# Where the extra transpositions of an attention slot stand: behind the turns, or between the dense tile and the values

## The chip, the cores and the metric

The kernel runs on one core of a Trainium2 chip. The metric is the device time of one execution in microseconds; the kernel before took 3290.62 us, the median of three runs (3289.79 to 3292.32).

## What is computed

The input is 4 sequences of 2048 tokens of width 512, in float32. Two residual blocks follow each other:

```python
x = x + layernorm(attention(layernorm(x), w_qkv))
x = x + layernorm(ffn(layernorm(x), ...))
```

The attention has 16 heads of width 32 and is local: a window of 128 queries sees its own 128 keys, those before and those after (384 keys, 256 at the two ends of a sequence):

```python
qkv = x @ w_qkv
scores = einsum('bhnqe,bhnke->bhnqk', q * E**-0.5, k_ctx)   # k_ctx: three neighbouring windows
out = einsum('bhnqk,bhnke->bhnqe', softmax(scores), v_ctx)
```

The feed-forward block mixes its weights for each sequence: a gate `g` is the mean over the tokens of `relu(x @ gate_w1.T + gate_b1) @ gate_w2.T + gate_b2`, and `W1 + sum_e g[e] * TW1[e]` (the same for W2 and the biases) is what the sequence is multiplied with, with a tanh-approximated GELU between. Only the attention part is touched by the change.

## The kernel before

**Two stages.** The first stage runs the attention, makes the normalized tokens of the second block (`xn2`) and writes them transposed to DRAM, and computes the gate. The second stage runs the feed-forward block. The mixing of the weights (`mixer`) is spread over both: it loads expert weights on SP's DMA queue (tile `exps`, four buffers, three ahead) and adds each to an accumulator with one VectorE (DVE) instruction.

**Slots.** The first stage is a loop over 256 slots (`for i in range(NS)`). There are 64 windows `W_` of 128 tokens, 16 a sequence, and 4 groups `g` of four heads each; slot `i` is window `i // 4`, group `i % 4`. The program is scheduled by hand: each engine executes its instructions in the order in which the Python code emits them, and waits only for data and for free buffers. One slot emits in this order:

1. `scores(i + 1)`: the scores of the next slot (L517), and on DVE their row maxima `nm` (L526).
2. In some slots a "fore" tile: one product of the query, key and value projection (`product`, L450) with its evacuation (`produced`). The projection of a block of 512 tokens is done with a seven-product scheme, spread over 12 slots, even products in `dense`, odd ones in `fore`.
3. `turn(i, j)` for the three (at sequence ends two) key blocks: four transpositions of probabilities each (tile `ptp`, L554) into a PSUM buffer, and a copy by ScalarE (ACT) to `prT` (L556).
4. `exponentials(i + 1)` on ACT (L539), in slots with a fore tile half of them ahead of it.
5. The entries of `mid[i]`: before the change only `pto`, in slots with `i % 4 == 0`. `out_transposes` (L248) turns the output of the window before back to token order; `out_scaled` normalizes it on DVE.
6. The entries of `rest[i]` (loads on SP, statistics and normalizations on DVE and POOL, stores on SP) and, from slot 84 on, 0 to 3 steps of the mixer (loads and stores on SP, L144 on DVE). Nothing here runs on TensorE (PE) or ACT.
7. The dense tile of the slot: either a projection product as above (`pm`, L450, PSUM pool `ps_m` with one buffer), or, in slots 12 to 15 of each 16, a tile of the gate (`pmg`, L163, four matmuls of 512 columns) whose ReLU with a sum runs on ACT (L168), or near the end of the stage an early piece of the feed-forward block (`pme`, L693). Evacuations are on ACT or DVE.
8. The first entry of `aux[i]`.
9. `values(i)`: 12 products with the values (tile `po`, L570) and a copy by ACT to `oT` (L577).
10. The further entries of `aux[i]`, then `late[i]`.

**What stands in aux.** Two kinds of transposition, of four PE instructions and one ACT copy each. `place_tile` (tile `pt_a`, L370, copied to `xnT`, L371) turns the normalized input of a coming block, in slots 12 to 15 of each 16. `via_pt(xn2_transposes, xn2_store, ...)` (tile `ptx`, L277, copied to `xo`, L282) turns `xn2` of a finished window, followed by its DMA store to `xT_d` on SP (L283); it comes in slots 0, 4, 8 and 11 of each 16, and at the end of the stage also in other slots. In no slot does `aux` hold more than one entry.

**Buffers.** All transposition tiles and `po` come from one PSUM pool with three buffers:

```python
ps_t = actx.enter_context(tc.tile_pool(name="ps_t", bufs=3, space=PSUM))
```

They are handed out in turn, so a tile waits until the third tile before it has been copied out. In a slot with three turns, `pto` and one aux entry the sequence is turn 0, turn 1, turn 2, `pto`, aux, `po`: `pto` takes the buffer of turn 0, the aux tile that of turn 1, `po` that of turn 2.

Of the kernel before, what the change touches and what calls it, by code (L numbers as in the profile page):

```python
# [34 lines left out]
def sandwich(ctx: ExitStack, tc: tile.TileContext, x, w_qkv, gw1, gb1, gw2, gb2, w1, b1, w2, b2, tw1, tb1, tw2, tb2, out):  # L35
    nc = tc.nc
# [226 lines left out]
    def residual(W_):  # L263
        st = win[W_]
        x1 = st["x1"]
        normalize(x1, st["a"], st["sb"])
        nc.vector.tensor_tensor(x1, x1, st["x"], ALU.add)
        nc.sync.dma_start(x1_d[W_], x1)
        st["sc"] = stats(x1, f"c{W_}")

    def normed(W_):
        st = win[W_]
        normalize(st["xn2"], st["x1"], st["sc"])
# [48 lines left out]
    with ExitStack() as actx:  # L322
# [6 lines left out]
        def load_tile(K, t, tag, bufs):  # L329
            b, k = divmod(K, NBLK)  # L330
            xt = qkvp.tile([P, D], F32, tag=tag, bufs=bufs, name=f"{tag}_{K}_{t}")
            nc.sync.dma_start(xt, x[b, k * TB + t * P : k * TB + (t + 1) * P])
            return xt
# [23 lines left out]
        def norm_stats(K, t):  # L357
            xs_of[K, t] = stats(x_of[K, t], f"a{K}_{t}")

        def norm_tile(K, t):  # L360
            xn = xn_of[K, t] = x_of.pop((K, t))
            normalize(xn, xn, xs_of.pop((K, t)))

        def place_tile(K, t, evac):
            if t == 0:
                xnT_of[K] = qkvp.tile([P, KC, TB], F32, tag="xnT", bufs=2, name=f"xnT_{K}")
            pt = ps_t.tile([P, KC, P], F32, tag="pt", name=f"pt_a{K}_{t}")
            xn = xn_of.pop((K, t))
            for kc in range(KC):
                nc.tensor.transpose(pt[:, kc, :], xn[:, ts(kc, P)], ident)  # L370
            evac(xnT_of[K][:, :, ts(t, P)], pt)  # L371
# [39 lines left out]
        def right_factors(K, part):  # L411

            x = xnT_of[K]
            r11, r12, r21, r22 = (x[:, 2 * i : 2 * i + 2, j * Q : (j + 1) * Q] for i in range(2) for j in range(2))
            if part == 0:
                t = wp.tile([P, 3, 2, Q], F32, tag="tx", name=f"tx_{K}")
                rights[K] = {"11": r11, "21": r21, "22": r22, "T1": t[:, 0], "T2": t[:, 1], "T3": r12, "T4": t[:, 2]}
                nc.vector.tensor_tensor(t[:, 0], r12, r11, ALU.subtract)
                nc.vector.tensor_tensor(t[:, 1], r22, t[:, 0], ALU.subtract)
            else:  # L420
                t = rights[K]
                nc.vector.tensor_tensor(r12, r22, r12, ALU.subtract)
                nc.vector.tensor_tensor(t["T4"], r21, t["T2"], ALU.subtract)
# [14 lines left out]
        def product(K, i, u, half, key=0):  # L438
            l, r, begins, _, _ = products[u]
            if begins and half == 0 and key:  # L440
                sc = ps_s.tile([P, 2, TB], F32, tag="sc", name=f"pm_{K}_{i}_{u}")
                bank[key] = sc[:, 0, :].rearrange("p (a b) -> p a b", a=2)
            elif begins and half == 0:
                bank[0] = ps_m.tile([P, 2, Q], F32, tag="pm", name=f"pm_{K}_{i}_{u}")
            if u < 2 and half == 0:
                rights.setdefault(K, {"11": xnT_of[K][:, :2, :Q], "21": xnT_of[K][:, 2:, :Q]})
            left, right = lefts[i][l], rights[K][r]
            for kc in range(2):
                a, b = (left, right) if i < 2 else (right, left)
                nc.tensor.matmul(  # L450
                    bank[key][:, half, :],
                    lhsT=a[:, kc, ts(half, P)],
                    rhs=b[:, kc, :],
                    start=(begins and half == kc == 0),
                    stop=True,
                    skip_group_check=True,
                )

        def produced(K, i, u, key=0):
            d = (q_of, k_of, v_of)[i]  # L460
            if u == 0:
                d[K] = projection(K, i)
            _, _, _, (row, col), added = products[u]
            if i == 2:
                row, col = col, row
            to = d[K][:, 2 * row : 2 * row + 2, col * Q : (col + 1) * Q]
            if added and i == 0:
                nc.vector.scalar_tensor_tensor(to, bank[key], QSCALE, to, ALU.mult, ALU.add)
            elif added:
                nc.vector.tensor_tensor(to, bank[key], to, ALU.add)  # L470
            elif i == 0:
                (nc.vector.tensor_scalar_mul if u == 3 else nc.scalar.mul)(to, bank[key], QSCALE)
            elif u == 3:
                nc.vector.tensor_copy(to, bank[key])
            else:
                nc.scalar.copy(to, bank[key])
# [103 lines left out]
        slots = range(-16, NS + 64)  # L580
        fore = {i: None for i in slots}
        dense = {i: None for i in slots}
        aux = {i: [] for i in slots}
        rest = {i: [] for i in slots}
        first = {i: [] for i in slots}
        mid = {i: [] for i in slots}
        late = {i: [] for i in slots}
        for K in range(1, NBK):
            s0 = 4 * (4 * K - 5)
            if K > 1:  # L590
                for t in range(WB):

                    i = s0 - 14 + 4 * t if K > 2 else s0 + t - 3
                    rest[i - 2].append(lambda K=K, t=t: x_of.__setitem__((K, t), load_tile(K, t, "x", 4)))
                    rest[i].append(lambda K=K, t=t: norm_stats(K, t))
                    rest[i + 1].append(lambda K=K, t=t: norm_tile(K, t))
                    aux[s0 + t].append(lambda K=K, t=t: place_tile(K, t, nc.scalar.copy))
            for part in range(2):
                rest[s0 + 4 + part].append(lambda K=K, part=part: right_factors(K, part))
            for i in range(3):  # L600
                for u in range(7):

                    (fore if u % 2 else dense)[s0 + 4 + 4 * i + (u + 1) // 2] = (
                        lambda half, K=K, i=i, u=u: product(K, i, u, half),
                        lambda K=K, i=i, u=u: produced(K, i, u),
                    )
# [11 lines left out]
        def gate_tile(K, oc, half):  # L618
            if half == 0:
                bank[0] = ps_m.tile([P, TB], F32, tag="pm", name=f"pmg_{K}_{oc}")  # L620
            gate_matmuls(bank[0], gT_of[K], oc, range(2 * half, 2 * half + 2))

        gate_at = {K: 4 * (4 * (K + 3) - 5) for K in range(11)} | {11: 204, 12: 220, 13: 236, 14: 248}
        for K, s0 in gate_at.items():
            first[s0 - 2].append(lambda K=K: load_gate(K))
            for oc in range(KC):
                dense[s0 + oc] = (
                    lambda half, K=K, oc=oc: gate_tile(K, oc, half),
# [25 lines left out]
        def via_pt(fill, use, W_, tag):  # L654
            pt = ps_t.tile([P, KC, P], F32, tag="pt", name=f"{tag}_{W_}")
            fill(W_, pt)
            use(W_, pt)

        for W_ in range(NWA - 1):
            mid[4 * W_ + 4].append(lambda W_=W_: via_pt(out_transposes, out_scaled, W_, "pto"))  # L660
            rest[4 * W_ + 5].append(lambda W_=W_: residual(W_))
            rest[4 * W_ + 6].append(lambda W_=W_: normed(W_))

            i = 4 * W_ + 8 if W_ < 58 and W_ % WB != 1 else 4 * W_ + 7
            aux[i].append(lambda W_=W_: via_pt(xn2_transposes, xn2_store, W_, "ptx"))

        first[240].append(lambda: load_first(0, 0, 0, wp, "w2"))
        first[240].append(lambda: load_first(0, 0, 1, wp, "w3"))
# [91 lines left out]
        for i in range(NS):  # L760
            W_, g = divmod(i, KC)
            nk = span_of(W_)[1]
            for f in first[i]:
                f()
            if i + 1 < NS:
                scores(i + 1)
            more = i + 1 < NS
            if fore[i]:
                fore[i][0](0)
                fore[i][0](1)  # L770
                if more:
                    exponentials(i + 1, (0, 1))
                fore[i][1]()
            for j in range(nk):
                turn(i, j)
            if more:
                exponentials(i + 1, (2, 3) if fore[i] else range(4))
            for f in mid[i]:
                f()

            for f in rest[i]:
                f()
            if i >= 84:
                for _ in range(MIXED[i % 16]):
                    next(blend)
            if dense[i]:
                dense[i][0](0)
                dense[i][0](1)
                dense[i][1]()
            for f in aux[i][:1]:  # L790
                f()
            values(i)
            for f in aux[i][1:] + late[i]:
                f()


# [371 lines left out]
```

## Time and profile before

| | us |
|---|---|
| median of three runs | 3290.62 |
| the profiled execution | 3291.22 |
| its span, first to last instruction | 3289.3 |
| PE busy, whole span | 3259.1 |
| stretch 60 to 1710 us (attention slots) | 1650.00 |
| PE busy in it | 1643.72 |
| DVE busy in it | 1281.49 |
| ACT busy in it | 1188.84 |
| POOL busy in it | 265.90 |

The groups of instructions that matter for the slots:

| line, engine, tile | count | busy us | mean ns |
|---|---|---|---|
| L554 PE, ptp | 2944 | 372.3 | 276 |
| L570 PE, po | 5888 | 214.8 | 277 |
| L517 PE, sc | 2816 | 245.1 | 422 |
| L163 PE, pmg | 480 | 215.9 | 592 |
| L556 ACT, prT | 736 | 385.8 | 594 |
| L539 ACT, exponentials | 1024 | 574.9 | 583 |
| L526 DVE, maxima | 512 | 449.9 | 919 |
| L144 DVE, mixer | 512 | 687.1 | 1342 |

A PE instruction's duration is longer than the step from one start to the next, since matmuls are pipelined and their ends are modelled; what a group of PE work costs is read from the start of it to the start of the next. "Idle before" is the time in which the engine did nothing, with the instruction or DMA that ended it. A float32 matmul shows as two PE records, so a dense tile of four matmuls is x8 in the timeline; a transposition is one record.

### The profile page before, as it was taken

To read this page: it belongs to the slowest core of one execution; us is meant where nothing else is said; L and a number is where in the kernel's file an instruction comes from. 1 tells how busy PE (TensorE), PEld (TensorE's weight loads), DVE (VectorE), ACT (ScalarE), POOL (GpSimd) and SP (SyncE) were. 2 spreads that over 40 slices of the span, in tenths; PEclk is the share of its full clock that TensorE was granted. 3 is DMA by queue.
4 is the path that set the end of the run, shared out by engine and by line. 5 is a ranking of instruction groups with operands and counts; after the bars stand their busy time and mean duration, and the time that the engine had idled before them with its cause. 6 is when DMAs were issued, how large, how long until landed. Compare 5 with 4: busy or idle time off the path is not lost.

```text
span 3289.3 us, 58549 instructions
## 1 busy us (share of the span) xinstructions
PE 3259.1 (99%) x22886; PEld 2627.5 (80%) x22886; DVE 2074.1 (63%) x2887; ACT 1572.6 (48%) x4212; POOL 722.5 (22%) x840
## 2 busy tenths in 40 slices
PE   9999999999999999999999999999999999999998
PEld 7777777777777777777768888888888888888887
DVE  5656555888888888888874665566556656412221
ACT  3777777677776777777771221122222122222121
POOL 1111111122221122111112322332322333321222
PEclk9999999999999999999999999999999999999999
DMA  2111111556665566656677789978788888732332
GB/s 85 50 62 49 43 52 53 169 193 202 215 214 181 193 203 213 196 177 204 232 264 270 259 288 329 334 284 298 273 320 319 304 287 302 278 109 90 128 128 78
DMA packets 316118, 651.96 MB, mean 198 GB/s; under 512 B 22969, under 2 KB 89657, under 8 KB 295490
## 3 DMA queue, kind: packets, MB, share of 16 engines
q1 hardware_dynamic: 315842, 648.22, 57.2%
q8 instruction: 180, 2.95, 0.4%
q14 instruction: 96, 0.79, 0.1%
HBM read 538.03 MB, written 110.10 MB: 197 GB/s over the span
## 4 chain that ended last, share of the span: by engine, by line
PE 95%; DVE 1%; DMA 1%; ACT 1%; POOL 1%; issue 0%; SPq 0%; DVEq 0%; ACTq 0%; POOLq 0%
PE pm L450 18%; PE px L817 13%; PE ptp L554 10%; PE px L915 9%; PE pz L915 7%; PE sc L517 7%; PE pz L817 6%; PE pmg L163 6%; PE po L570 6%; PE py L915 3%; PE py L817 3%; PE py2b L915 3%; PE pto L248 1%; DMA exps<-in_tw 1%; PE ptx L277 1%; PE pt_a L370 1%
## 5 line engine op out<-in xcount | busy, mean ns | idle before, releaser
L144 DVE SCALAR_TENSOR_TENSOR acc<-exps,g,acc 128x1024 f32<-128x1024 f32 x512 | 687.1, 1342 | 185.5 <-DMA exps<-in_tw 179.6
L539 ACT ACTIVATE pr<-sc,nm 128x384 f32<-128x384 f32 (+1 forms) x1024 | 574.9, 583 | 218.3 <-DVE nm L526 218.3
L526 DVE TENSOR_REDUCE nm<-sc 128x2 f32<-128x768 f32 (+1 forms) x512 | 449.9, 919 | 279.7 <-PE sc L517 277.8
L556 ACT COPY prT<-ptp 128x512 f32<-128x512 f32 x736 | 385.8, 594 | 164.6 <-PE ptp L554 159.9
L994 ACT ACTIVATE y<-y,shift,rs_d 128x512 f32<-128x512 f32 x64 | 52.0, 813 | 742.8 <-POOL shift L993 742.8
L554 PEld LDWEIGHTS ptp<-ident,pr 128*128 128x128 f32 x2944 | 329.6, 141 | 54.2 <-issue 32.9
L554 PE MATMUL ptp<-ident,pr 128*128 128x128 f32 x2944 | 372.3, 276 | 0.0
L817 PE MATMUL px<-tT,w 128*128 128x256 f32 x1512 | 349.9, 379 | 1.9 <-ACT cpb L868 1.9
L817 PEld LDWEIGHTS px<-tT,w 128*128 128x128 f32 x1512 | 286.7, 190 | 42.4 <-ACT cpb L868 3.3
L517 PE MATMUL sc<-k,q 32*128 32x384 f32 (+2 forms) x2816 | 245.1, 422 | 5.2 <-ACT pr L539 5.0
L874 DVE TENSOR_TENSOR cpb<-pz,cpb 128x512 f32<-128x512 f32 x63 | 43.5, 691 | 326.3 <-PE pz L817 285.6
L92 POOL TENSOR_SCALAR ve_b<-mv_b 128x1 f32<-128x1 f32 x64 | 47.1, 737 | 837.8 <-DVE mv_b L90 837.8
L915 PE MATMUL px<-w2s,u 128*128 128x256 f32 x1024 | 228.9, 379 | 0.7 <-ACT last L282 0.7
L539 ACT ACTIVATION_READ_ACCUMULATOR pr<-sc,nm 128x1 f32 x1024 | 224.0, 219 | 0.0
L915 PEld LDWEIGHTS px<-w2s,u 128*128 128x128 f32 x1024 | 194.5, 190 | 27.3 <-ACT last L282 0.9
L163 PE MATMUL pmg<-gT,gw_sb 128*128 128x512 f32 x480 | 215.9, 592 | 0.0
L570 PE MATMUL po<-prT,v 128*32 128x128 f32 x5888 | 214.8, 277 | 0.1
L570 PEld LDWEIGHTS po<-prT,v 128*32 128x32 f32 x5888 | 145.3, 109 | 71.1 <-issue 56.8
L892 POOL TENSOR_TENSOR t<-u 128x512 f32<-128x512 f32 x64 | 84.0, 1312 | 503.0 <-ACT u L829 487.1
L450 PE MATMUL pm<-xnT,wqkv 128*128 128x256 f32 x744 | 183.3, 389 | 0.0
L517 PEld LDWEIGHTS sc<-k,q 32*128 32x128 f32 x2816 | 120.0, 183 | 60.7 <-issue 45.5
L450 PEld LDWEIGHTS pm<-xnT,wqkv 128*128 128x128 f32 x744 | 134.9, 191 | 41.6 <-ACT oT L577 22.3
(169 smaller groups left out, 5310.3 us busy)
## 6 DMA issues: line engine op xcount, KB each, us to landing
exps<-in_tw SPq DMA_DIRECT2D x512, 512.0 KB, 5.9
w2s<-m2d SPq DMA_DIRECT2D x112, 1024.0 KB, 6.4
acc<-in_w SPq DMA_DIRECT2D x64, 512.0 KB, 6.7
x<-in_x SPq DMA_DIRECT2D x64, 256.0 KB, 3.0
m1d<-acc SPq DMA_DIRECT2D x64, 256.0 KB, 6.1
m2d<-acc SPq DMA_DIRECT2D x64, 256.0 KB, 6.9
w<-m1d SPq DMA_DIRECT2D x16, 1024.0 KB, 8.2
fxT<-xTd SPq DMA_DIRECT2D x16, 1024.0 KB, 9.0
```

What stands on the lines that cost most here:

```text
L144: nc.vector.scalar_tensor_tensor(acc, ets.pop(n), g_all[b][:, e : e + 1], acc, ALU.mult, ALU.add)
L163: nc.tensor.matmul(pm, lhsT=gw1_sb[:, kc, ts(oc, P)], rhs=xT[:, kc, :], start=(kc == 0), stop=(kc == KC - 1))
L450: nc.tensor.matmul(bank[key][:, half, :], lhsT=a[:, kc, ts(half, P)], rhs=b[:, kc, :], start=(begins and half == kc == 0), stop=True, skip ...
L517: nc.tensor.matmul(scs[r // 2][:, r % 2, col : col + nj * W], lhsT=q[rows, g, ts(W_ % WB, W)], rhs=k_of[kb][rows, g, j0 * W : (j0 + nj) * ...
L526: nc.vector.tensor_reduce(st["nm"][:, h : h + 2], scs[u][:, :, : nk * W], AX.X, ALU.max, negate=True)
L539: nc.scalar.activation(pr[:, : nk * W], scs[r // 2][:, r % 2, : nk * W], AF.Exp, bias=st["nm"][:, h : h + 1], accum_out=st["den"][:, h : h ...
L554: nc.tensor.transpose(pt[:, r, :], st["pr"][g * 4 + r][:, ts(j, W)], ident)
L556: nc.scalar.copy(prT, pt)
L570: nc.tensor.matmul(po[r * E : (r + 1) * E, 0, :], lhsT=v_of[kb][:, jj, h * E : (h + 1) * E], rhs=prT[:, r, :], start=(j == 0), stop=(j == ...
L817: nc.tensor.matmul(bank[:, f, :], lhsT=factor[:, f, kc * P : (kc + 1) * P], rhs=right[:, kc, :], start=(start and f == 0 and kc == 0), sto ...
L892: nc.gpsimd.tensor_tensor(t1s[c], b12, us[c][:, :, :Q], ALU.subtract)
L915: nc.tensor.matmul(bank[:, t, :], lhsT=right(c - c % 2)[:, c % 2, ts(t, P)], rhs=w[:, c, :], start=(start and c == t == 0), stop=True, ski ...
```

## The change

The dictionary `aux` is gone. `place_tile` and the `xn2` transposition with its copy and its store now stand in `mid[i]`, so they are emitted after the turns and the exponentials, ahead of `rest[i]`, the mixer's steps and the dense tile. In slots that have `pto` as well, `pto` is put at the head of `mid[i]`, so it stays the first tile behind the turns. After the dense tile `values(i)` follows directly. The instructions are the same ones, and the three PSUM buffers are handed out in the same sequence.

```diff
-        aux = {i: [] for i in slots}
...
-                    aux[s0 + t].append(lambda K=K, t=t: place_tile(K, t, nc.scalar.copy))
+                    mid[s0 + t].append(lambda K=K, t=t: place_tile(K, t, nc.scalar.copy))
...
         for W_ in range(NWA - 1):
-            mid[4 * W_ + 4].append(lambda W_=W_: via_pt(out_transposes, out_scaled, W_, "pto"))
+            mid[4 * W_ + 4].insert(0, lambda W_=W_: via_pt(out_transposes, out_scaled, W_, "pto"))
             rest[4 * W_ + 5].append(lambda W_=W_: residual(W_))
             rest[4 * W_ + 6].append(lambda W_=W_: normed(W_))
 
             i = 4 * W_ + 8 if W_ < 58 and W_ % WB != 1 else 4 * W_ + 7
-            aux[i].append(lambda W_=W_: via_pt(xn2_transposes, xn2_store, W_, "ptx"))
+            mid[i].append(lambda W_=W_: via_pt(xn2_transposes, xn2_store, W_, "ptx"))
...
                 dense[i][0](0)
                 dense[i][0](1)
                 dense[i][1]()
-            for f in aux[i][:1]:
-                f()
             values(i)
-            for f in aux[i][1:] + late[i]:
+            for f in late[i]:
                 f()
```

On PE the moved transpositions pass the slot's dense tile. On ACT their copy passes the evacuation of the dense tile, where that is on ACT. On SP the store of `ptx` passes the DMAs that `rest[i]` and the mixer issue in that slot. On DVE and POOL the order is unchanged.

## The prediction

> **What bounds the kernel.** First the page's rows of busy time and the chain of work that ended last:
>
> ```profile
> PE 3259.1 (99%) x22886; PEld 2627.5 (80%) x22886; DVE 2074.1 (63%) x2887; ACT 1572.6 (48%) x4212; POOL 722.5 (22%) x840
> ...
> PE 95%; DVE 1%; DMA 1%; ACT 1%; POOL 1%; issue 0%; SPq 0%; DVEq 0%; ACTq 0%; POOLq 0%
> ```
>
> TensorE runs 3259.1 of 3289.3 us and is 95% of the chain. The table of stretches narrows it to where the diff acts: from 60 to 1710 us (the attention slots) PE is busy 1643.72 of 1650.00 us, ACT 1188.84, DVE 1281.49. So in these slots a nanosecond between the start of one PE group and the start of the next is a nanosecond of the kernel, and nothing else is, unless it makes PE wait. I therefore read PE's timeline, start to start. Columns: start, duration, engine, line, operation, tiles, shape, count.
>
> ```profile
> 1022.41 1.53 PE L554 MATMUL ptp<-ident,pr 128*128 128x128 f32 x12
> 1023.80 0.66 PE L248 MATMUL pto<-ident,oT 128*128 128x128 f32 x4
> 1024.30 1.89 PE L450 MATMUL pm<-xnT,wqkv 128*128 128x256 f32 x8
> 1026.03 0.60 PE L277 MATMUL ptx<-ident,x 128*128 128x128 f32 x4
> 1026.56 0.86 PE L570 MATMUL po<-prT,v 128*32 128x128 f32 x24
> ...
> 1030.04 1.47 PE L554 MATMUL ptp<-ident,pr 128*128 128x128 f32 x12
> 1031.35 1.89 PE L450 MATMUL pm<-tx,wsum 128*128 128x256 f32 x8
> 1033.17 0.86 PE L570 MATMUL po<-prT,v 128*32 128x128 f32 x24
> ```
>
> The second slot has no extra transposition: twelve turn transpositions take 1.31 us (0.109 each), the dense tile 1.82 up to the values. In the first slot, dense to ptx takes 1.73 and ptx to the values 0.53: together 2.26, that is 1.82 and 0.44, four times 0.109. **Where it stands now, the second transposition costs its bare 0.44 us.** The one behind the turns (pto) does not: turns to pto 1.39, pto to dense 0.50.
>
> **What such a place costs.** Two parts can be read off. The tile pto takes the PSUM buffer of turn 0, so it waits for ACT's copy of turn 0:
>
> ```profile
> 1023.16 0.59 ACT L556 COPY prT<-ptp 128x512 f32<-128x512 f32 x1 [1.21 <-PE ptp L554]
> ...
> 1026.83 0.63 ACT L476 COPY k<-pm 128x512 f32<-128x512 f32 x1
> 1027.30 0.65 ACT L282 COPY xo<-ptx 128x512 f32<-128x512 f32 x1
> ```
>
> The copy ends at 1023.75, pto starts at 1023.80. Slots of the same kind with no pto take 1.37 for the turns (median 1.367 over 36; with pto 1.391 over 56): the wait is 0.024 us. Then, having waited, the first transposition starts with its weights unloaded: pto to the next group is 0.493 (median over 44), 0.056 over four times 0.109. So a charge of **0.080 us** where the first buffer is waited for. For a tile behind pto the trace has the very order of the changed kernel once, in slot 12, which has no dense tile, and for a tile directly behind the turns in slot 13:
>
> ```profile
> 131.12 1.53 PE L554 MATMUL ptp<-ident,pr 128*128 128x128 f32 x12
> 132.51 0.66 PE L248 MATMUL pto<-ident,oT 128*128 128x128 f32 x4
> 133.00 0.65 PE L370 MATMUL pt_a<-ident,x 128*128 128x128 f32 x4
> 133.59 0.86 PE L570 MATMUL po<-prT,v 128*32 128x128 f32 x24
> ...
> 136.60 1.53 PE L554 MATMUL ptp<-ident,pr 128*128 128x128 f32 x12
> 137.99 0.66 PE L370 MATMUL pt_a<-ident,x 128*128 128x128 f32 x4
> ```
>
> pto to pt_a is 0.49, as pto to a dense tile: no added wait (ACT's copy of turn 1 lands just in time). pt_a to the values is 0.59 (0.584), against 0.53 where the tile stands behind dense: a charge of **0.056**. In slot 13 turns to pt_a is again 1.39: wait and restart both, 0.080.
>
> Last, the dense tile now runs straight into the values. In gate slots:
>
> ```profile
> 1081.70 1.53 PE L554 MATMUL ptp<-ident,pr 128*128 128x128 f32 x12
> 1083.07 3.60 PE L163 MATMUL pmg<-gT,gw_sb 128*128 128x512 f32 x8
> 1086.50 0.60 PE L370 MATMUL pt_a<-ident,x 128*128 128x128 f32 x4
> 1087.03 0.86 PE L570 MATMUL po<-prT,v 128*32 128x128 f32 x24
> ...
> 1610.02 3.60 PE L163 MATMUL pmg<-gT,gw_sb 128*128 128x512 f32 x8
> 1613.55 0.86 PE L570 MATMUL po<-prT,v 128*32 128x128 f32 x24
> ```
>
> Gate to values directly 3.53; gate to pt_a 3.44 plus pt_a to values 0.53 is 3.97, again 0.44 more. The 0.09 of entering the values is paid once in both orders; the change saves nothing there.
>
> **The sum.** The moved tiles are 56 pt_a (K from 2 to 15) and 63 ptx, at most one to a slot.
> - 40 slots with ptx and 10 with pt_a behind pto, three key blocks: 50 x 0.056 = 2.8.
> - 30 gate slots with pt_a alone, 15 slots 11 (of each 16) with ptx alone, 2 late ptx in gate slots: 47 x 0.080 = 3.8.
> - 6 edge slots with two key blocks and pto: pto takes an old buffer (no charge there: 0.44), so the next tile waits for turn 0's copy, by its time 0.51 us after the last turn started about 0.02 too late: 6 x 0.080 = 0.5.
> - Nothing: 9 edge slots without pto (buffer long free), 4 early slots without a dense tile (order unchanged), 2 late slots in which PE waits for ACT anyway, and the last ptx.
>
> Together 7.0 us (2.8 + 3.8 + 0.5, unrounded). Against the profiled execution: span 3289.3 to 3296.3, its time 3291.22 to 3298.2. That execution lies 0.6 above the median of 3290.62, so I forecast the median at 3290.6 + 7.0 = **3297.6 us**, +0.21%.
>
> **What else moves, at nothing, and its cover.** *ACT:* the copy of the moved tile now stands ahead of the dense tile's copy (k, q, v, or the gate's ReLU). In slots 0, 4 and 8 the next slot's fore tile needs that one PSUM buffer. ACT leaves the exponentials at 1026.83, so xo takes 1026.83 and k starts at 1027.30 and ends at 1027.93; the fore tile starts at 1028.21 now, 1028.26 then. Cover about 0.3 us; if it went, at most the 0.47 of a copy in 40 slots, 19 us. In gate slots the copy fills ACT's idle time before the ReLU. *SP:* the store of xT waits for the xo copy, and now stands ahead of the loads that rest and the mixer issue. In slot 11 a load of exps that is issued at 1067.05 goes out behind the store, at about 1073.3. Its user is the second multiply-add of slot 12, at 1079.20; these loads take 4.7 us at the median from issue to landing and 9.7 at most up to 1720 us, so 5.9 usually suffices. If not, DVE has 1.32 us idle before the next maxima and these lead the exponentials by over a microsecond. In slots 4 and 8 the user comes two slots later. *DVE, POOL:* nothing moved. *Values:* they still start after the third turn copy, under the dense tile.
>
> **Two rules against rows.** The Trainium skill, "TensorE: Matmul & The Clock Gate", section "LDWEIGHTS (loading the stationary operand)", prices a load at its columns over 1.2 GHz, 107 ns for 128. A load that can't be pulled ahead of the matmul before it would then show in full: 103 x 0.107 + 53 x 0.024 = 12.3 us, 3302.9. The row of pto shows 0.056 exposed; the row decides, and 12.3 sets my upper end. The same page, "Part 4: PE-mode transpose", says that transpositions don't count as activity for the clock gate, which speaks against gathering them: a window at half clock costs some 1.7 us, in 100 slots 170. But slot 12 already runs 131.12 to 133.59, twenty transpositions, at granted clock 1.00 (stretch 131.2 to 134.6). The clock does fall to 0.50 from 148.3 to 151.7, after slots without dense tiles and with PE waiting 0.65; the changed slots keep dense tile and no gap. By the row: nothing.
>
> **Rivals.**
> 1. *No charge* (not slower): if turn 0's copy ended 0.08 us sooner relative to the turns, the tile's weights would load under the last turn and the move would be order only: 3290.6. For it: the edge slots' pto with its old buffer pays 0.44. Against it: 56 pto all wait to within 5 ns of each other, and the buffers are handed out in an unchanged sequence (turns, pto, moved tile, values). A gain has no row: no step of today's order pays anything that vanishes.
> 2. *Late mixer loads:* decides when a landing in slot 11 passes 5.9 + 2.7 = 8.6 us. At 10 us, 1.4 us each in 14 slots: 7 + 20, 3317.
> 3. *Fore tile waits for the swapped ACT copy:* decides over 0.3 us; 0.2 us beyond in 40 slots: +8, 3305.6.
> 4. *Clock gate:* 3290.6 + 170, some 3460.
>
> **How the numbers follow.** Forecast 0.75, rival 1 0.12, rival 2 0.04, rival 3 0.07, rival 4 0.02. About 0.2% (6.6 us) is what can be told from no change here. The forecast is 0.4 us beyond that; the runs of before spread by 2.5 us, and two half-clock windows (at 148 and 1640 us) fall where they will, worth about 1 us each. So of the forecast's 0.75 some 0.48 lies over the bound and 0.27 under it. Slower: 0.48 + 0.13 = 0.61; same: 0.27 + 0.10 = 0.37; faster 0.02. The range 3294 to 3303 reaches from half the charge to the rule's price and leaves out rival 1 and the large ones.
>
> **What would show it.** In the changed trace: turns to a lone moved tile 1.39 in gate slots and about 1.34 in slot 11; pto to ptx 0.49; moved tile to dense 0.49; dense to values 1.82 and 3.53 everywhere; DVE's waits for exps not grown from 41 us before 1990 us. I am wrong if moved tile to dense is 0.44, if the fore tile starts over 0.90 us after the scores, or if DVE's lateness reaches PE.

## The result, and the profile after

The changed kernel takes 3312.52 us, the median of five runs (3310.95 to 3313.53), against 3290.62 (3288.71 to 3292.32) of the kernel before: a ratio of 1.0066, with a 95% interval of 1.0055 to 1.0077. It is slower by 21.9 us. The forecast was 3297.6, slower by 7.0, with a range of 3294 to 3303. The direction was right; 15 us were missing. The busy time and the chain of the changed kernel, from its page:

```profile
PE 3270.8 (99%) x22886; PEld 2620.7 (79%) x22886; DVE 2069.4 (63%) x2887; ACT 1570.3 (47%) x4212; POOL 720.9 (22%) x840
...
PE 95%; DMA 2%; DVE 2%; ACT 1%; POOL 0%; issue 0%; SPq 0%; DVEq 0%; ACTq 0%; POOLq 0%
```

The span grew by 21.4 us and PE's busy time by 11.7 alone, so about half of the loss is time in which PE stood still. The chain has DMA and DVE at 2% each, where before both had 1%: two things on it that PE now waits for.

To find the places, the slots of both traces are laid side by side, each from the start of its scores to the start of the next. Most slots differ by what was forecast. PE's timeline of the changed kernel, a slot with pto and ptx and a gate slot (start, duration, engine, line, operation, tiles, shape, count):

```profile
1035.50 1.53 PE L554 MATMUL ptp<-ident,pr 128*128 128x128 f32 x12
1036.89 0.66 PE L248 MATMUL pto<-ident,oT 128*128 128x128 f32 x4
1037.38 0.65 PE L277 MATMUL ptx<-ident,x 128*128 128x128 f32 x4
1037.87 1.89 PE L450 MATMUL pm<-xnT,wqkv 128*128 128x256 f32 x8
1039.69 0.86 PE L570 MATMUL po<-prT,v 128*32 128x128 f32 x24
...
1095.02 1.53 PE L554 MATMUL ptp<-ident,pr 128*128 128x128 f32 x12
1096.41 0.66 PE L370 MATMUL pt_a<-ident,x 128*128 128x128 f32 x4
1096.91 3.60 PE L163 MATMUL pmg<-gT,gw_sb 128*128 128x512 f32 x8
1100.44 0.86 PE L570 MATMUL po<-prT,v 128*32 128x128 f32 x24
```

Turns to pto 1.39, pto to ptx 0.49, ptx to dense 0.49, dense to values 1.82; in the gate slot 1.39, 0.50 and 3.53. Each is the forecast step. Added over all changed slots the charge is 6.9 us.

The other 14.5 us of the 21.4 by which the span grew lie in two places, and a remainder. Slot 85 takes 15.81 us in place of 6.61 (+9.2). Slots 241 and 242 together take 4.2 us longer. The feed-forward stage takes 1.0 us longer. The rest cancels to about 0.1: the first slots, where the half-clock windows fall elsewhere, and slots 78 and 160, where a late ACT copy costs 0.28 each.

**Slot 85.** PE's timeline of the changed kernel there:

```profile
610.23 1.47 PE L554 MATMUL ptp<-ident,pr 128*128 128x128 f32 x12
618.20 3.78 PE L450 MATMUL pm<-tx,wsum 128*128 128x256 f32 x8 [6.50 <-DVE k L470]
621.91 1.51 PE L570 MATMUL po<-prT,v 128*32 128x128 f32 x24
```

The dense tile starts 7.97 us after the turns (1.31 elsewhere): PE waits 6.50 us for DVE, which should have taken the fore tile out of the one projection buffer. DVE's timeline says why it is late:

```profile
606.20 0.18 DVE L90 BATCH_NORM_AGGREGATE mv_b<-st_b 128x2 f32<-128x6 f32 x1
614.54 1.28 DVE L144 SCALAR_TENSOR_TENSOR acc<-exps,g,acc 128x1024 f32<-128x1024 f32 x1 [8.15 <-DMA exps<-in_tw]
615.74 1.81 DVE L526 TENSOR_REDUCE nm<-sc 128x2 f32<-128x768 f32 x2
617.47 0.68 DVE L470 TENSOR_TENSOR k<-pm,k 128x512 f32<-128x512 f32 x1
```

It stood 8.15 us before the mixer's very first multiply-add, and the row maxima and the copy of k are queued behind that. In the kernel before the same instruction began 0.10 us after the one ahead of it started, without a wait:

```profile
604.37 1.27 DVE L144 SCALAR_TENSOR_TENSOR acc<-exps,g,acc 128x1024 f32<-128x1024 f32 x1
```

The multiply-add waits for expert weights. ACT's copy of ptx and SP's timeline in the changed kernel, then SP's in the kernel before:

```profile
606.97 0.62 ACT L282 COPY xo<-ptx 128x512 f32<-128x512 f32 x1
```

```profile
607.62 0.52 SPq L283 DMA_DIRECT2D xTd<-xo  x1
608.24 0.58 SPq L332 DMA_DIRECT2D x<-in_x  x1
608.86 0.45 SPq L116 DMA_DIRECT2D acc<-in_w  x1
609.36 2.15 SPq L119 DMA_DIRECT2D exps<-in_tw  x4
```

```profile
595.09 0.40 SPq L332 DMA_DIRECT2D x<-in_x  x1
595.54 0.42 SPq L116 DMA_DIRECT2D acc<-in_w  x1
596.02 2.00 SPq L119 DMA_DIRECT2D exps<-in_tw  x4
606.18 0.53 SPq L283 DMA_DIRECT2D xTd<-xo  x1
```

Slot 84 is the first in which the mixer runs, and it has a ptx. Before, SP had run ahead of the other engines and issued the first loads at 596.02, some eight microseconds before their use at 604.37; then it waited for the xo copy, with nothing behind it that was urgent. Now the store stands ahead, and its wait for the xo copy (which ends at 607.59) holds the first loads back until 609.36, 3.0 us after DVE was ready for them at 606.39.

**Slots 241 and 242.** In slot 242 the first piece of the feed-forward block waits for its input. PE's timeline, of the kernel before and of the changed one, then SP's of the changed one and of the kernel before:

```profile
1639.78 2.73 PE L554 MATMUL ptp<-ident,pr 128*128 128x128 f32 x12
1642.31 2.40 PE L693 MATMUL pme<-fxT,w 128*128 128x512 f32 x4
```

```profile
1656.60 1.53 PE L554 MATMUL ptp<-ident,pr 128*128 128x128 f32 x12
1661.59 3.43 PE L692 MATMUL pme<-fxT,w 128*128 128x512 f32 x4 [3.46 <-DMA fxT<-xTd]
```

```profile
1642.88 0.52 SPq L283 DMA_DIRECT2D xTd<-xo  x1
1643.49 0.57 SPq L119 DMA_DIRECT2D exps<-in_tw  x1
...
1645.98 3.11 SPq L119 DMA_DIRECT2D exps<-in_tw  x2
1649.18 0.89 SPq L309 DMA_DIRECT2D w<-m1d  x2
1650.13 0.42 SPq L291 DMA_DIRECT2D fxT<-xTd  x1
```

```profile
1628.09 0.53 SPq L283 DMA_DIRECT2D xTd<-xo  x1
1628.70 1.07 SPq L309 DMA_DIRECT2D w<-m1d  x2
1629.83 0.42 SPq L291 DMA_DIRECT2D fxT<-xTd  x1
```

SP's rows of the changed kernel are slot 239: its store, then the mixer's loads and stores of that slot, then the loads that slot 240 issues for the feed-forward block. Before, the mixer's loads were out by the time of the store, and fxT followed it by 1.7 us (1628.09 and 1629.83). Now it follows by 7.2, since everything of slot 239 must pass between them. The load itself took about as long as before, 11.3 us from issue to landing against 10.4. PE's wait is 3.46 us. The 4.2 us are this wait and a shift of half-clock windows, in which PE was granted half its clock: the changed kernel has one in slot 241 and one that reaches past the wait in slot 242, the kernel before had one in slot 242 as well (1639.9 to 1643.3), which is why its rows above are long.

### The profile page after: what moved, and what is told of

It reads as the page before. It is cut to its first block, busy times and chain, and to the rows that moved or that the text cites. A ratio compares the mean times of both kernels' runs of the same rounds, so it can differ in the third digit from the quotient of the medians.

```text
span 3310.7 us, 58580 instructions
## 1 busy us (share of the span) xinstructions
PE 3270.8 (99%) x22886; PEld 2620.7 (79%) x22886; DVE 2069.4 (63%) x2887; ACT 1570.3 (47%) x4212; POOL 720.9 (22%) x840
## 4 chain that ended last, share of the span: by engine, by line
PE 95%; DMA 2%; DVE 2%; ACT 1%; POOL 0%; issue 0%; SPq 0%; DVEq 0%; ACTq 0%; POOLq 0%
PE pm L450 18%; PE px L814 13%; PE ptp L554 10%; PE px L912 9%; PE pz L912 7%; PE sc L517 6%; PE pz L814 6%; PE pmg L163 6%; PE po L570 6%; PE py L912 3%; PE py L814 3%; PE py2b L912 3%; DMA exps<-in_tw 1%; PE ptx L277 1%; PE pto L248 1%; PE pt_a L370 1%
```

## The experiments

The theory after the result: the loss is 6.9 us of charge on PE and two stalls made by one DMA store's new place on SP. The rival: the new order on PE and ACT makes the stalls (the dense tile and its copy come later and hold up the fore tile, which is what PE's wait "for DVE k" looks like at first sight), or half-clock windows that fall elsewhere do.

**Only the store goes back.**

```diff
         nc.scalar.copy(xo, pt)
-        nc.sync.dma_start(xT_d[K][:, :, ts(w, P)], xo)
+        if W_ == NWA - 1:
+            xn2_put(W_)
+
+    def xn2_put(W_):
+        K, w = divmod(W_, WB)
+        nc.sync.dma_start(xT_d[K][:, :, ts(w, P)], win[W_]["xo"])
         del win[W_]
...
             mid[i].append(lambda W_=W_: via_pt(xn2_transposes, xn2_store, W_, "ptx"))
+            put[i].append(lambda W_=W_: xn2_put(W_))
...
                 dense[i][1]()
+            for f in put[i]:
+                f()
             values(i)
```

> The changed kernel, but the store of ptx's copy is issued on SP where it stood before, behind the dense tile; transpositions and ACT copies stay moved. Theory (SP's queue: the store holds up the mixer's first loads in slot 84 and those ahead of the first feed-forward block in slot 239): both stalls go, 9.2 + 4.2 + 1.0 us less, leaving the charge of the transpositions, 6.9 us: 3297.5 (3296 to 3299). Rival (order on PE and ACT: the dense tile and its copy come later and hold up the next slot): the stalls stay, 3311 to 3313.

Measured: 3298.84 us against 3291.24, ratio 1.0023 (1.0014 to 1.0031). Both stalls are gone. PE and SP of this kernel around slots 84 and 85:

```profile
610.88 1.47 PE L559 MATMUL ptp<-ident,pr 128*128 128x128 f32 x12
612.19 1.89 PE L455 MATMUL pm<-tx,wsum 128*128 128x256 f32 x8
614.01 0.86 PE L575 MATMUL po<-prT,v 128*32 128x128 f32 x24
```

```profile
598.59 2.27 SPq L119 DMA_DIRECT2D exps<-in_tw  x4
608.28 0.53 SPq L288 DMA_DIRECT2D xTd<-xo  x1
```

Turns to dense is 1.31 again, with PE and ACT in the changed order. The order on PE and ACT makes no stall; what remains, 7.6 us (4.6 to 10.2 by the interval), agrees with the charge of 6.9.

**The mixer's first loads one slot earlier.** Everything stays changed; a `yield` behind the first three loads, and slot 83 takes that step.

```diff
         for n in range(3):
             load(n)
+        yield
...
+        rest[83].append(lambda: next(blend))
```

> The changed kernel, all transpositions and stores moved, but the mixer's first three loads are issued one slot earlier, in slot 83, ahead of the store of slot 84. Theory (SP's queue): slot 85 is 6.6 us long again, 9.2 less: 3303.3 (3302 to 3304.5); the stall before the feed-forward block stays. Rival (order on PE and ACT): slot 85 stays at 15.8 us, 3312.5. Rival (the first loads are just slow, whatever stands before them): slot 85 gains the same 6.6 us, so this run tells it apart only with e1.

Measured: 3304.58 us, ratio 1.0040 (1.0027 to 1.0052), just over the upper end that was expected. Slot 85 is back at 6.61 us, the first multiply-add no longer waits, and slot 242 still stalls (PE waits 4.09 us for fxT). DVE's timeline of this kernel:

```profile
606.31 1.27 DVE L145 SCALAR_TENSOR_TENSOR acc<-exps,g,acc 128x1024 f32<-128x1024 f32 x1
```

Together with the run above: it is the loads' place behind the store, not their own length.

**The ptx of slot 239 alone goes back.**

```diff
-            mid[i].append(lambda W_=W_: via_pt(xn2_transposes, xn2_store, W_, "ptx"))
+            (aux if i == 239 else mid)[i].append(lambda W_=W_: via_pt(xn2_transposes, xn2_store, W_, "ptx"))
...
+            for f in aux[i]:
+                f()
             values(i)
```

What the expectation calls slots 244 and 245 are slots 241 and 242.

> The changed kernel with the single ptx of slot 239 back between the dense tile and the values. Theory (its store stands ahead of three loads of the mixer, which wait for DVE, and behind them the loads of the first feed-forward block): slots 244 and 245 lose 4.2 us of stall, 0.08 of charge goes: 3308.2 (3307 to 3309.5), slot 85 still 15.8 us. Rival (half-clock windows that fall elsewhere): slots 244 and 245 stay longer by over 2 us, 3311 or more.

Measured: 3305.98 us, ratio 1.0042 (1.0028 to 1.0056), 2.2 us below what was expected and 1 us below the range. In its trace slot 242's dense tile follows the turns at 1.37 with no wait, as it should:

```profile
1655.92 1.53 PE L554 MATMUL ptp<-ident,pr 128*128 128x128 f32 x12
1657.29 1.88 PE L693 MATMUL pme<-fxT,w 128*128 128x512 f32 x4
```

The rest of the difference is not shown to be the store: the kernel before has a half-clock window in slot 242 which this run has not, so that slot is 1.7 us shorter than even before, and the feed-forward stage is 0.9 us shorter than before; slot 85, on the other hand, is 10.1 us longer than before here. The stall in slot 242 is shown to come from slot 239's store; its size alone is known to a microsecond or two.

**One ptx moved, in slot 84.** The kernel before, with `mid if i == 84 else aux` for ptx (in this kernel ptx stands ahead of pto in that slot).

> The kernel before with one tile moved: the ptx of slot 84, where the mixer starts. Theory (the mixer's first loads wait behind its store, and its first multiply-add holds DVE and with it the row maxima): slot 85 takes some 15.8 us in place of 6.6, + 9.2 us and 0.06 of charge: 3300.5 (3299 to 3302) against 3291.2. Rival (the stall needs the whole change, as a phase that has built up over 84 slots): 3291.3.

Measured: 3301.28 us against 3292.26, ratio 1.0026 (1.0016 to 1.0036): +9.0. PE's timeline of this kernel has the same wait in slot 85:

```profile
615.57 3.78 PE L450 MATMUL pm<-tx,wsum 128*128 128x256 f32 x8 [7.29 <-DVE k L470]
```

Moving one tile of 119 costs at least about as much as the charge of all the others.

**Only place_tile moved.** No DMA changes its place.

> The kernel before with only place_tile moved behind the turns; no DMA is moved. Theory (a charge of 0.080 for a lone tile that waits for turn 0's copy, 0.05 behind pto, none where the buffer is old): 30 x 0.08 + 10 x 0.05 + 3 x 0.08 = 3.1 us: 3293.7 (3292.5 to 3295). Rival (the charge is an artefact of where the records start): 3290.6, same as before.

Measured: 3294.78 us, ratio 1.0011 (1.0005 to 1.0018): +3.5. By slots: 0.080 in the gate slots with pt_a alone, 0.05 behind pto, 0.08 in the edge slots behind pto, and 0.00 in the nine edge slots where the tile takes an old buffer. The same move costs nothing where there is no fresh buffer to wait for: the charge is the wait for turn 0's or turn 1's copy and the restart after it, not the neighbourhood of transpositions. PE's weight loads (PEld) in the kernel before show the restart. A tile that waits begins its first load only when its first transposition begins, pto at 1023.80; behind the dense tile ptx begins it 0.22 us ahead of its transposition at 1026.03:

```profile
1023.80 0.42 PEld L248 LDWEIGHTS pto<-ident,oT 128*128 128x128 f32 x4
1025.81 0.57 PEld L277 LDWEIGHTS ptx<-ident,x 128*128 128x128 f32 x4
```

**The opposite: pto behind the dense tile too.** If a transposition behind the turns pays for a fresh buffer, then pto pays already before the change.

```diff
-            mid[4 * W_ + 4].append(lambda W_=W_: via_pt(out_transposes, out_scaled, W_, "pto"))
+            aux[4 * W_ + 4].insert(0, lambda W_=W_: via_pt(out_transposes, out_scaled, W_, "pto"))
```

with all of `aux[i]` ahead of `values(i)`.

> The opposite of the change: the kernel before with pto moved from behind the turns to behind the dense tile, ahead of the other tile and the values; its DVE work then stands behind the mixer's. Theory (a transposition behind the turns waits for turn 0's copy and restarts, 0.080 in 56 slots with three key blocks; behind the dense tile it costs its bare 0.44): 4.5 us less, 3286.7 (3285.5 to 3289) against 3291.2, turns to dense 1.31 or 1.37, dense to pto 1.73 or 3.44. Rival (the first transposition behind a dense tile always pays, or DVE's normalization comes too late for the next slot's turn 0, which takes its buffer): no gain or slower, 3291 to 3296.

Measured: 3287.04 us against 3292.26, ratio 0.9986 (0.9980 to 0.9993): 5.2 us faster than the kernel before, and faster than all others here. In its trace the slots with pto and three key blocks are 0.08 shorter each; the seven edge slots with pto, where its buffer is old, are unchanged. A slot of it:

```profile
1019.16 1.53 PE L554 MATMUL ptp<-ident,pr 128*128 128x128 f32 x12
1020.53 1.89 PE L450 MATMUL pm<-xnT,wqkv 128*128 128x256 f32 x8
1022.26 0.60 PE L248 MATMUL pto<-ident,oT 128*128 128x128 f32 x4
1022.70 0.60 PE L277 MATMUL ptx<-ident,x 128*128 128x128 f32 x4
1023.23 0.86 PE L570 MATMUL po<-prT,v 128*32 128x128 f32 x24
```

Turns to dense 1.37, dense to pto 1.73, pto to ptx 0.44: no charge for either tile. DVE now waits for pto, 53.7 us in 56 slots, but waits that much less for the next scores (224.6 in place of 277.8), and the next slot's turns don't wait for it.

## Why the prediction was right in one part and wrong in the sum

**Right: the charge on PE.** Forecast 7.0, measured 6.9 in the trace (7.6 in the times, with the store put back), so the direction was not luck. Wait and restart for a lone tile 0.080, restart behind pto 0.05 to 0.06, dense to values 1.82 and 3.53, nothing saved. That slot 12 and slot 13 of the kernel before held the new order already made this possible. To take the whole load of 107 ns, from the Trainium skill ("TensorE: Matmul & The Clock Gate", section "LDWEIGHTS (loading the stationary operand)"), as exposed was too much: the charge would have been 12.3 us, and the trace has 0.056 for each.

**Right: ACT and the clock gate.** After a slot with ptx the fore tile starts 0.86 us after the scores, as before. The slots with twenty transpositions in a row did not lower the clock: from 632 to 1644 us of the changed kernel it is 1.00. **Right: rival 1** (no charge) did not come about.

**Wrong: the step "What else moves, at nothing, and its cover", in its part on SP.** It named the mechanism (the store waits for the xo copy, and the mixer's loads stand behind it) and rival 2 gave it a price, but both were worked out in slot 11, in the steady state, and for the other slots it said: "In slots 4 and 8 the user comes two slots later." In slot 84, a slot 4, this does not hold. The mixer starts there, no load is ahead, and the first load's user is in the same slot. The step that should have been made: not the typical load behind the moved store, but each one, the first first. An estimate from the kernel before: the xo copy passes the k copy, so the store goes out 0.46 us sooner, at about 605.7 in place of 606.18; the store, the loads of x and of the accumulator take 0.6, 0.45 and 0.48 before the first load is out, at about 607.2; with the median of 4.7 us it lands at 611.9; its user was ready at 604.4. That is 7.5 us late; 8.15 were measured. Of this the slot paid 6.66 between turns and dense tile, and 2.5 more because PE's clock had fallen, below. The sign that the prediction named for it, DVE's waits for expert weights in sum, would have hidden this: 41.1 us before and 43.4 after, while the longest single wait went from 5.4 to 8.2. The sign "DVE's lateness reaches PE" did show it.

**Wrong: what else stands behind the mixer's loads.** The step counted the mixer's loads and not those of the next slots. `first[240]` issues the inputs of the feed-forward block, and these wait behind slot 239's loads, which now stand behind the store: PE waits 3.46 us for them, and slots 241 and 242 take 4.2 us longer in all.

The upper end of the range had come from the 12.3 us, a larger charge; the real excess was of another kind. The extra 1.0 us in the feed-forward stage isn't explained: across these runs that stage differs from the kernel before by -0.9 to +4.0 us, with half-clock windows at different places, and nothing here ties it to the change.

## What to carry to other kernels

When an instruction is moved in a queue that is worked off in order, list all that it is moved past, up to the next slot, and look first at where a pipeline starts: in slot 84 the prefetch distance had become zero, and a wait that was free in nearly all other slots was paid there in full. In this kernel the store, which waits for late data, belongs behind the loads of its slot. A tile here that takes a PSUM buffer filled just before it waits for the copy (0.024 us) and shows part of its weight load as well (0.056); a dense tile of 1.7 us between the two removed both.

## What the runs showed that was not expected

The stall of PE cost more than its wait. The table of stretches shows the changed kernel in the stall of slot 85, at its end with what follows, and after that (length, then busy time of PE, PEld, DVE, ACT and POOL with counts, then the granted clock, the DMA share and GB/s):

```profile
610.30:616.60 6.30, 1.40 (x13) 1.16 (x11) 2.06 (x2) 0.00 (x0) 0.00 (x0) 1.00 1.04 386
616.80:623.40 6.60, 5.20 (x36) 3.56 (x36) 4.54 (x7) 4.33 (x12) 1.73 (x2) 0.50 0.54 168
624.00:630.00 6.00, 6.00 (x57) 4.82 (x52) 5.39 (x8) 4.42 (x12) 1.90 (x2) 1.00 0.19 72
```

For most of the wait the clock is still at 1.00. It falls some 1.5 us before PE starts again at 618.20, and the whole stretch from 616.80 to 623.40 has 0.50, so the dense tile takes 3.71 us in place of 1.82 and the values 1.44 in place of 0.79. Of the 9.2 us that slot 85 lost, 2.5 are this. The wait in slot 242 is followed by the same: from 1661.20 to 1664.40 the clock is 0.50, and the dense tile takes 3.36 us in place of 1.81. A long wait is not the only thing that comes before such a window: the kernel before has one at 1639.9, with no wait of PE over 0.7 us in the 15 us before it. What sets these windows is not shown here.
